# Four-stage network on one core: keys of two heads in one strip, a norm of a norm without its own moments, counts as thresholds, and a new order of the front

## The chip, the cores and the metric

The kernel runs on one core of a Trainium2 chip. The metric is the device time of the whole program in microseconds (us); lower is better. The core has five engines that run beside each other and wait for one another by semaphores: TensorE (PE; its weight loads are listed apart as PEld), VectorE (DVE), ScalarE (ACT), GpSimd (POOL) and SyncE (SP), which issues DMAs.

## The reference

The input is 16 sequences of 256 tokens with 128 features. Four blocks follow each other, each with a residual and a layer norm on both sides; `_layernorm` has no gain.

```python
x = x + _layernorm(_L0_attn_ref(_layernorm(x), ...))   # block 1: layer norm with gain, 16 heads of 8, MLP
x = x + _layernorm(_L0_ffn_ref(_layernorm(x), ...))    # block 2: dense MLP plus product-key experts
x = x + _layernorm(_L1_attn_ref(_layernorm(x), ...))   # block 3: 16 heads of 8, output bias
x = x + _layernorm(_L1_ffn_ref(_layernorm(x), ...))    # block 4: six layers of local attention and MLP
```

Block 1 begins with a second layer norm of what the first gives, so that a norm of a norm is computed. In block 2 each token has, for each of 4 query heads, two lists of 64 scores; the 8 best of each list are taken, the 64 sums of pairs are formed, the 8 best sums are kept, and the 8 experts with the indices `ix * 64 + iy` are mixed by a softmax of these sums. All arithmetic is fp32 in the reference.

## The kernel before

Blocks 1 to 3 are one software pipeline, called the front here; block 4 is another, which starts when the front has ended. A sequence lies as two tiles of 128 tokens, on partitions, by 128 features. The front's work on one sequence is cut into 177 named steps. The string `FRONT` lists them as `name:lag`. The loop `run` goes through this list once a pass; in pass number s it executes each step for sequence s minus its lag, if there is one. The text calls one pass a step of the pipeline where it gives times. With 16 sequences and a largest lag of 11 there are 27 passes. The class `InOrder` makes every engine run its instructions in exactly this order, and all instructions made through it carry the line of its helper, L46. So each engine has a queue of its own in the order of the list, and an instruction starts when those in front of it on its engine and those it needs are done.

The names, with the engine of each:

- La to Lh are the eight layer norms. `.a` takes the moments on DVE (two `bn_stats`, two `bn_aggr`), `.b` makes scale and offset on POOL (four instructions on 2 elements), `.c` applies them on ACT, `.d` adds to the residual on POOL. La and Lb are the two norms in front of block 1. Lc is inside block 1, Ld behind it; Le and Lf stand around block 2, Lg and Lh around block 3.
- A and C are the attentions of blocks 1 and 3. Small letters are PE, capitals what takes the result out of PSUM: q and k project, Q and K copy out on ACT, m and s are score products (each for 4 or 2 groups of heads; m finds the maxima, s is done again with the negated maxima added as a row), M is the maximum on DVE, n transposes the maxima on PE, N adds them to the queries on DVE, E is the exponential on ACT, c is the product with the values, C copies it on ACT, t and x transpose on PE, T divides by the sum on DVE, X copies on ACT, o is the output product.
- tA, tM, tB, tC are transposes on PE, TA to TC copies on ACT; h, H, mo, my is block 1's MLP (PE, ACT with Gelu, PE, DVE), hs the sum in front of it (DVE); xo and hb add bias rows on POOL; Cy adds the bias of block 3 on DVE.
- Block 2: S (PE) and Z (ACT) make the scores, r0 and r1 take the 8 best of each list on DVE (tiles `mx`, `mi`), r2 casts the indices (`mf`) and forms the sums of pairs, r3 takes the 8 best sums, shifts their places right by 3 (`pk<-pk`), casts them (`pa<-pk`) and subtracts the largest; r4 is the exponential on ACT, r5 the sum of it on DVE. r6 and r7 mark, by comparing and adding on 4096 elements a partition, the rank of each second index in `rt`; r8 counts for each first index how many partners were kept, and writes a threshold for each into `rt` (tiles `at`, `cnt`, `nb`, `thr`); r9 does the case of an index past the end (`far`, `pl`). b, B transpose `rt`; d multiplies with a constant matrix `sel`, and D keeps an expert's weight where the product is above a constant (tile `w`). ys and X0, X1 on POOL form the weights of all 512 experts from the scores (`exy<-sim,mx`; `w<-exy`, one for each tile of tokens), ye is the exponential on ACT between them. w multiplies with the experts' inner products on DVE (`w<-w,hh`), W applies Silu on ACT, l corrects one element on POOL, g, G, o, oy give the output; u, U, f, F are the dense products.

The 16 heads lie in four groups of four strips. A strip is 32 partitions, holds one head's 8 rows of keys or queries, and row `NMROW` takes the maxima.

## Time and profile before

| what | value |
|---|---|
| median of 3 runs | 4587.18 us (4584.28 to 4592.25) |
| the profiled execution | 4579.81 us, of which the span from first to last instruction is 4578.0 us |
| busy in the span | PE 93%, PEld 68%, DVE 73%, ACT 70%, POOL 67% |
| granted clock of TensorE | 0.973 of full speed |
| end of the front | the last residual sum of block 3, `x<-x,Lhy` on POOL, starts at 1250.61 us |

The page cuts the span into 40 slices, in each of which a digit gives an engine's busy share in tenths. The chain of waits goes back from the last instruction to what released each; the groups put instructions of one shape together, with the number, the busy time and the mean duration; the timeline lists instructions of one engine by start and duration. A duration in it includes time in which an instruction has been started and is held up, and the start of one may lie before the end of the one in front.

### The profile page before, as it was taken

Reading aid. Unit: us, or ns where it says so; the run is one execution under the profiler, and the core shown is the slowest. Engines: PE = TensorE matmul, PEld = TensorE weight load, DVE = VectorE, ACT = ScalarE, POOL = GpSimd, SP = SyncE. Lnnn points to the kernel's source line nnn. Section 1 sums busy time; section 2 is a strip of 40 time slices with the busy share of each in tenths; the row PEclk is TensorE's granted clock in tenths of the full one; section 3 lists DMA queues with packets and bytes.
Section 4 is the critical chain, followed back from the end, with each engine's and each line's share of the span. In section 5 each row is a group of like instructions: output and inputs, shape, how many; then the busy total and the mean of one; then the engine's idle time right before and its main releaser. Section 6 shows DMA issues by size and latency. Waiting matters only on the chain.

```text
span 4578.0 us, 169228 instructions
## 1 busy us (share of the span) xinstructions
PE 4275.8 (93%) x74304; PEld 3123.8 (68%) x74304; DVE 3334.8 (73%) x5376; ACT 3197.5 (70%) x5919; POOL 3072.3 (67%) x2858
## 2 busy tenths in 40 slices
PE   7799999998668999999999999999999999999997
PEld 5567676676435767777777777777777777777776
DVE  3899999998546776777767677776767777676774
ACT  2576676776467777777777777777777777777775
POOL 3343443443357887778777777778777787878885
PEclk9899999999879999999999999999999999999998
DMA  2000000000022322223232222323232232323231
GB/s 50 1 2 3 2 2 2 2 2 2 13 65 66 78 71 70 71 70 76 66 74 68 73 73 67 75 68 78 66 74 67 73 75 68 71 59 78 70 73 50
DMA packets 220132, 242.03 MB, mean 53 GB/s; under 512 B 95777, under 2 KB 126578, under 8 KB 219250
## 3 DMA queue, kind: packets, MB, share of 16 engines
q1 hardware_dynamic: 215170, 229.10, 20.4%
q8 instruction: 584, 9.57, 0.9%
q10 hardware_dynamic: 4224, 2.10, 0.2%
q14 instruction: 154, 1.26, 0.1%
...
## 4 chain that ended last, share of the span: by engine, by line
PE 64%; DVE 17%; ACT 12%; issue 2%; POOL 2%; DMA 1%; SPq 1%; ACTq 0%; POOLq 0%; DVEq 0%
PE pp L46 22%; PE po L46 11%; PE sc L46 6%; PE ph L46 6%; PE pt L46 5%; PE pc L46 5%; PE pe L46 3%; DVE m L46 3%; ACT qT L46 2%; DVE nmA L46 2%; ACT eT L46 2%; PE s L46 2%; ACT v L46 2%; ACT cT L46 2%; ACT xn L46 2%
## 5 line engine op out<-in xcount | busy, mean ns | idle before, releaser
L46 PE MATMUL pp<-part,xT 128*128 128x512 f32 x2304 | 1103.4, 609 | 18.3 <-ACT cT L46 9.7
L46 POOL TENSOR_TENSOR am<-a,r 128x1024 f32<-128x1024 f32 x384 | 730.2, 1902 | 435.1 <-PE pt L46 211.9
L46 POOL TENSOR_TENSOR a<-a 128x512 f32<-128x512 f32 x768 | 960.2, 1271 | 11.9 <-DVE a L46 11.9
L46 DVE TENSOR_TENSOR a<-pp,tab 128x2048 f32<-128x2048 f32 x384 | 877.6, 2285 | 118.8 <-POOL am L46 83.1
L46 PEld LDWEIGHTS pp<-part,xT 128*128 128x128 f32 x2304 | 404.7, 192 | 361.6 <-issue 300.5
L46 DVE TENSOR_TENSOR e<-sc,m_win 128x1024 f32<-128x1024 f32 x192 | 235.1, 1224 | 473.1 <-PE sc L46 469.8
L46 ACT COPY kT<-pt 128x512 f32<-128x512 f32 x384 | 229.1, 597 | 446.3 <-PE pt L46 443.8
L46 DVE TENSOR_REDUCE sm<-e 128x16 f32<-128x1024 f32 x192 | 233.2, 1215 | 382.3 <-ACT e L46 382.3
L46 POOL TENSOR_TENSOR e<-e,mx 128x1024 f32<-128x1024 f32 x192 | 365.1, 1901 | 208.1 <-DVE mx L46 202.7
L46 PEld LDWEIGHTS pt<-ident,am 128*128 128x128 f32 x3072 | 353.3, 141 | 204.8 <-issue 150.3
L46 PE MATMUL pt<-ident,am 128*128 128x128 f32 x3072 | 466.0, 279 | 25.5 <-POOL am L46 22.0
L46 ACT ACTIVATE sq<-pp 128x1024 f32<-128x1024 f32 x384 | 396.0, 1032 | 99.0 <-PE pp L46 69.0
L46 DVE TENSOR_REDUCE r<-sq 128x16 f32<-128x1024 f32 x384 | 455.9, 1208 | 0.0
...
L46 PEld LDWEIGHTS po<-wo,cT 128*128 128x128 f32 x3200 | 376.8, 193 | 57.6 <-issue 45.1
...
L46 PE MATMUL po<-wo,cT 128*128 128x128 f32 x3200 | 382.5, 277 | 5.2 <-ACT cT L46 5.2
L46 POOL TENSOR_TENSOR e<-e,sm 128x1024 f32<-128x1024 f32 x192 | 365.3, 1903 | 5.5 <-DVE sm L46 5.5
...
L46 ACT COPY eT<-pe 128x512 f32<-128x512 f32 x384 | 224.7, 585 | 78.5 <-PE pe L46 78.5
...
## 6 DMA issues: line engine op xcount, KB each, us to landing
...
```

What stands on the lines that cost most here:

```text
L46: ins = trace(*args, **kw)
```

## The change

Keys: the two halves of the heads share strips. A strip now holds the keys of two heads, in rows 0 to 7 and 8 to 15, and the maxima's row moves to 16. The key projection has two groups in place of four, and so have its copies out of PSUM. The queries keep four groups; each head's 8 rows stand at the place of its key, and the other 8 are zero, so a score product of 32 rows gives one head's scores.

The second norm: Lb no longer takes moments. The mean of a normed row is zero and its variance follows from La's moments and scale; Lb.b computes scale and offset from these with six instructions on POOL, and Lb.c applies them to `x` instead of to the first norm's result.

Thresholds: r8 writes the count itself into `rt`, as the result of its last reduce. The instruction that formed 8 minus the count is gone. `sel` has plus one where it had minus one, and D compares with 8.5 instead of 0.5.

Order: r3 is cut in two, and the shift, the cast and the subtraction become r3b, which stands behind Lf.a. The list `FRONT` is new: the lags are mostly larger by 3 or 4, since the list begins at another place of the pass, and several steps have moved against each other: among others w0 behind Le.a, W0 in front of Z0, Cs1 behind S1, ye behind oy, Lf.c behind AE0, and X1 behind Lf.d and La.b and ahead of Lg.b.

```diff
@@ -25,7 +25,9 @@
 NH = 16
 DH = 8
-NMROW = 8
+NMROW = 16
 RH, NK, NE, TOP = 4, 64, 512, 8
@@ -119,32 +121,31 @@
             )
         return m
-    def in_strips(self, pool, name, src, scale=1.0):
-        w = pool.tile([128, 4, 4, 32], FP, name=name)
+    def in_strips(self, pool, name, src, keys, scale=1.0):
+        w = pool.tile([128, 2 if keys else 4, 4, 32], FP, name=name)
         self.nc.gpsimd.memset(w, 0.0)
-        self.nc.vector.tensor_scalar(
-            w.rearrange("p g j s -> p (g j) s")[:, :, 0:DH],
-            src.rearrange("p (h e) -> p h e", e=DH),
-            scale,
-            None,
-            ALU.mult,
-        )
+        src = src.rearrange("p (k s j e) -> p s k j e", k=2, s=2, e=DH)
+        for s in range(2):
+            dst = w if keys else w.rearrange("p (k s) j r -> p s k j r", s=2)[:, s]
+            self.nc.vector.tensor_scalar(dst[:, :, :, DH * s : DH * s + DH], src[:, s], scale, None, ALU.mult)
         return w.rearrange("p g j s -> p g (j s)")
     FRONT = """
-F0:8 Lf.d:9 r7:8 Lg.a:9 Ak0:6 As2:7 r4:8 F1:8 Ak2:6 Ct0:10 AK0:6 Lg.b:9 AK2:6 r8:8 AE2:7 Ac0:7
-        Ct1:10 X1:8 Am0:6 Lb.c:5 Lh.c:11 CT0:10 AC0:7 r5:8 CT1:10 r9:8 Lg.c:9 Ac2:7 AM0:6 AC2:7 Lh.d:11 Av:6
-        tA:5 b0:8 AV:6 TA:5 b1:8 Cx:10 B0:8 At0:7 B1:8 AT0:7 CX:10 d02:8 At1:7 d00:8 D02:8 d10:8 AT1:7 D00:8
-        d13:8 D10:8 Am2:6 D13:8 tC:9 Ax:7 TC:9 AM2:6 Co:10 Cy:10 AX:7 d03:8 Ao:7 hs:7 Am1:6 D03:8 d12:8
-        Lc.a:7 Lc.b:7 D12:8 d01:8 Ck0:9 d11:8 La.c:4 CK0:9 D01:8 Cq0:9 Lc.c:7 tM:7 CQ0:9 D11:8 TM:7 Ck2:9
-        La.b:2 w0:8 Cq2:9 CK2:9 AM1:6 CQ2:9 h0:7 h2:7 Cm0:9 Cv:9 H0:7 w1:8 H2:7 mo:7 hb:7 W0:8 CM0:9 xo:5
-        CV:9 Cm1:9 my:7 Ld.a:7 u2:8 CM1:9 Ld.b:7 An0:6 l0:8 U2:8 AN0:6 Ld.c:7 Ld.d:7 An2:6 Le.a:7 Cm2:9
-        Cn0:9 Aq0:5 Le.b:7 W1:8 AN2:6 CN0:9 CM2:9 Lb.a:4 Le.c:7 AQ0:5 Aq2:5 tB:7 La.a:0 TB:7 Cs1:9 S0:7
-        AQ2:5 l1:8 S1:7 Z0:7 Cn2:9 Z1:7 Lh.a:10 Lb.b:4 CN2:9 r0:7 r1:7 g0:8 g1:8 r2:7 r6:7 CE1:9 G0:8 Cs0:9
-        G1:8 ys:7 o:8 CE0:9 oy:8 Lh.b:10 Cs2:9 CE2:9 u0:7 Lf.a:8 Cc0:9 U0:7 Cc2:9 Lf.b:8 ye:7 r3:7 As1:6
-        X0:7 AE1:6 f0:7 CC0:9 As0:6 Lf.c:8 CC2:9 AE0:6 f1:7
+        CM0:13 An2:10 Cv:13 W1:12 Cm1:13 my:11 Aq0:9 Ld.a:11 AN2:10 u2:12 Ld.b:11 CV:13 Ld.c:11 Aq2:9 CM1:13
+        Cm2:13 AQ0:9 Ld.d:11 U2:12 Le.a:11 w0:12 AQ2:9 Le.b:11 Le.c:11 CM2:13 tB:11 TB:11 Cn0:13 S0:11 l1:12
+        W0:12 S1:11 CN0:13 La.a:0 Z0:11 Cn2:13 Z1:11 Cs1:13 l0:12 Lh.a:14 CN2:13 r0:11 CE1:13 g0:12 g1:12
+        Lh.b:14 G0:12 r1:11 G1:12 Cs0:13 r2:11 Lh.c:14 r3:11 CE0:13 o:12 Cs2:13 u0:11 oy:12 ys:11 ye:11
+        Lf.a:12 Cc0:13 CE2:13 U0:11 Cc2:13 As1:10 r3b:11 r6:11 r4:11 X0:11 r5:11 Lf.b:12 CC0:13 f0:11 AE1:10
+        f1:11 r7:11 F0:11 As0:10 CC2:13 Ct0:13 Ct1:13 CT0:13 CT1:13 F1:11 AE0:10 Ak0:9 As2:10 Ak2:9 Lf.c:12
+        Lf.d:12 tA:8 AK0:9 r8:11 Ac0:10 AK2:9 Av:9 La.b:5 AE2:10 TA:8 Lb.c:7 Am0:9 Lg.a:12 AC0:10 Ac2:10
+        AV:9 r9:11 AM0:9 b0:11 AC2:10 X1:11 Cx:13 B0:11 b1:11 Lb.b:5 d02:11 CX:13 D02:11 At0:10 AT0:10 B1:11
+        At1:10 AT1:10 La.c:8 d13:11 d10:11 Lg.b:12 xo:8 D13:11 d00:11 Lg.c:12 D10:11 Am2:9 tC:12 Ax:10 TC:12
+        D00:11 Co:13 Ck0:12 AX:10 AM2:9 Ao:10 hs:10 Am1:9 CK0:12 Cy:13 Lc.a:10 d03:11 Ck2:12 CK2:12 Lc.b:10
+        D03:11 Lc.c:10 d12:11 D12:11 d01:11 d11:11 Cq0:12 hb:10 CQ0:12 D01:11 D11:11 tM:10 TM:10 AM1:9
+        Cq2:12 h0:10 CQ2:12 h2:10 w1:11 An0:9 H0:10 AN0:9 Cm0:12 H2:10 Lh.d:14 mo:10
...
@@ -182,7 +183,7 @@
         a = w["A"] = {
             "qb": self.load(wp, "qb", ins["q_b"], [128, 4]),
-            "kb": self.load(wp, "kb", ins["k_b"], [128, 4]),
+            "kb": self.load(wp, "kb", ins["k_b"], [128, 2]),
         }
         nc.vector.tensor_scalar(a["qb"], a["qb"], DH**-0.5, None, ALU.mult)
         w["f1"] = wp.tile([128, 4, 128], FP, name="f1")
@@ -208,7 +209,7 @@
                     a["wv"] = wp.tile([128, 128], FP, name="wv")
                     nc.vector.tensor_copy(a["wv"], p)
                 else:
-                    a[f"w{k}"] = self.in_strips(wp, f"w{k}", p, DH**-0.5 if k == "q" else 1.0)
+                    a[f"w{k}"] = self.in_strips(wp, f"w{k}", p, k == "k", DH**-0.5 if k == "q" else 1.0)
             u = self.load(fp, "uo", ins["out_U"], [96, 128])
             v = self.load(fp, "vo", ins["L0_attn_out_V"], [96, 128])
             p = ps.tile([128, 128], FP, name="p", tag="f")
@@ -247,14 +248,14 @@
             c = w["C"] = {
                 "qb": None,
-                "kb": self.load(wp, "no_kb", ins["no_kb"], [128, 4]),
+                "kb": self.load(wp, "no_kb", ins["no_kb"], [128, 2]),
                 "ob": self.load(wp, "bo", ins["L1_attn_bo"].partition_broadcast(128), [128, D]),
                 "wv": self.load(wp, "wv3", ins["L1_attn_Wv"], [128, 128]),
                 "wo": self.load(wp, "wo3", ins["L1_attn_Wo"], [128, 128]),
             }
             for k in "qk":
                 raw = self.load(fp, f"raw{k}", ins[f"L1_attn_W{k}"], [128, 128])
-                c[f"w{k}"] = self.in_strips(wp, f"w3{k}", raw, DH**-0.5 if k == "q" else 1.0)
+                c[f"w{k}"] = self.in_strips(wp, f"w3{k}", raw, k == "k", DH**-0.5 if k == "q" else 1.0)
         w["up"] = self.load(wp, "wup", ins["W_up"], [128, 512])
         w["dn"] = self.load(wp, "wdn", ins["W_down"].rearrange("(c p) d -> p c d", p=128), [128, 4, D])
         w["de"] = self.load(wp, "de", ins["down_embed"], [128, NE])
@@ -271,9 +272,7 @@
         sel = w["sel"] = wp.tile([128, 8, NK], BF, name="sel")
         nc.vector.tensor_copy(sel[0:64], self.ident_bf[0:64, 0:64].unsqueeze(1).to_broadcast([64, 8, NK]))
-        nc.vector.tensor_scalar(
-            sel[64:72], self.ident_bf[64:72, 64:72].unsqueeze(2).to_broadcast([8, 8, NK]), -1.0, None, ALU.mult
-        )
+        nc.vector.tensor_copy(sel[64:72], self.ident_bf[64:72, 64:72].unsqueeze(2).to_broadcast([8, 8, NK]))
         w["m_q"] = self.mask(wp, "m_q", [128, 4, 128], [(0, 1, [[0, 4], [-1, 128]])])
         w["m_k"] = self.mask(wp, "m_k", [128, 4, 128], [(0, -1, [[0, 4], [1, 128]])])
@@ -333,7 +332,7 @@
             @op(name + ".a")
             def _(n):
                 st = small(name + "st", [2, 6])
-                mv = put(n, (name, "mv"), small(name + "mv", [2, 2]))
+                mv = put(n, (name, "mv"), small(name + "mv", [2, 2], bufs=6))
                 src = source(n)
                 for t in range(2):
                     nc.vector.bn_stats(st[:, t, :], src[:, t, :])
@@ -343,8 +342,8 @@
             @op(name + ".b")
             def _(n):
                 mv = get(n, (name, "mv"))
-                rstd = put(n, (name, "rstd"), small(name + "rstd", [2]))
-                off = put(n, (name, "off"), small(name + "off", [2]))
+                rstd = put(n, (name, "rstd"), small(name + "rstd", [2], bufs=6))
+                off = put(n, (name, "off"), small(name + "off", [2], bufs=6))
                 nc.gpsimd.tensor_scalar(rstd, mv[:, :, 1], EPS, None, ALU.add)
                 nc.gpsimd.tensor_tensor(rstd, rstd, self.half.to_broadcast([128, 2]), ALU.pow)
                 nc.gpsimd.tensor_scalar(off, mv[:, :, 0], -1.0, None, ALU.mult)
@@ -369,7 +368,21 @@
                 nc.gpsimd.tensor_tensor(x_of(n), x_of(n), get(n, name + "y"), ALU.add)
         norm("La", x_of, tile_as("x0", 3))
-        norm("Lb", lambda n: get(n, "x0"), tile_as("x1", 2, "turned"))
+        norm("Lb", x_of, tile_as("x1", 2, "turned"))
+        @op("Lb.b")
+        def _(n):
+            mv, first = get(n, ("La", "mv")), get(n, ("La", "rstd"))
+            scale, off = put(n, ("Lb", "rstd"), small("Lbrstd", [2])), put(n, ("Lb", "off"), small("Lboff", [2]))
+            r = small("Lbr", [2])
+            nc.gpsimd.tensor_tensor(r, mv[:, :, 1], first, ALU.mult)
+            nc.gpsimd.tensor_tensor(r, r, first, ALU.mult)
+            nc.gpsimd.tensor_scalar(r, r, EPS, None, ALU.add)
+            nc.gpsimd.tensor_tensor(r, r, self.half.to_broadcast([128, 2]), ALU.pow)
+            nc.gpsimd.tensor_tensor(scale, first, r, ALU.mult)
+            nc.gpsimd.tensor_tensor(off, get(n, ("La", "off")), r, ALU.mult)
         norm("Lc", lambda n: get(n, "hs"), tile_as("x2", 2, "turned"))
         norm("Ld", lambda n: get(n, "y"), tile_as("Ldy"))
         norm("Le", x_of, tile_as("xn", 2, "turned"))
@@ -418,8 +431,8 @@
                         r = slice(32 * j, 32 * j + 32)
                         nc.tensor.matmul(
                             s[:, i, o : o + 128],
-                            lhsT=lhs[r, g, lcols],
-                            rhs=rhs[r, g, rcols.start + o : rcols.start + o + 128],
+                            lhsT=lhs[r, g * lhs.shape[1] // 4, lcols],
+                            rhs=rhs[r, g * rhs.shape[1] // 4, rcols.start + o : rcols.start + o + 128],
                             start=False,
                             stop=i == m - 1 and o == 512 // m - 128,
                         )
@@ -430,16 +443,15 @@
             nm, va = a["nm"], a["va"]
             pairs = {"0": 0, "2": 2}
-            def projected(n, g, weights, name):
-                p = put(n, (k + name, g), bank("p" + name, [2, SEQ]))
-                for i in range(2):
-                    nc.tensor.matmul(
-                        p[:, i, :], lhsT=weights[:, g + i, :], rhs=get(n, "xT" + k), start=True, stop=True
-                    )
+            def projected(n, g, weights, name, m):
+                p = put(n, (k + name, g), bank("p" + name, [m, SEQ]))
+                for i in range(m):
+                    lhsT = weights[:, g * m // 2 + i, :]
+                    nc.tensor.matmul(p[:, i, :], lhsT=lhsT, rhs=get(n, "xT" + k), start=True, stop=True)
             @by(k + "q", pairs)
             def _(n, g):
-                projected(n, g, a["wq"], "q")
+                projected(n, g, a["wq"], "q", 2)
             @by(k + "Q", pairs)
             def _(n, g):
@@ -455,16 +467,14 @@
             @by(k + "k", pairs)
             def _(n, g):
-                projected(n, g, a["wk"], "k")
+                projected(n, g, a["wk"], "k", 1)
             @by(k + "K", pairs)
             def _(n, g):
                 if g == 0:
-                    put(n, k + "kT", pool.tile([128, 4, SEQ], FP, name="kT" + k))
+                    put(n, k + "kT", pool.tile([128, 2, SEQ], FP, name="kT" + k))
                 kT, p = get(n, k + "kT"), get(n, (k + "k", g))
-                for i in range(2):
-                    bias = a["kb"][:, g + i : g + i + 1]
-                    nc.scalar.activation(kT[:, g + i, :], p[:, i, :], AF.Identity, bias=bias)
+                nc.scalar.activation(kT[:, g // 2, :], p[:, 0, :], AF.Identity, bias=a["kb"][:, g // 2 : g // 2 + 1])
             @op(k + "v")
             def _(n):
@@ -710,6 +720,11 @@
             for g in range(G):
                 nc.vector.max(sc[:, g, :], pairs[:, g, :])
                 nc.vector.max_index(pk[:, g, :], sc[:, g, :], pairs[:, g, :])
+            put(n, "pk", pk), put(n, "sc", sc)
+        @op("r3b")
+        def _(n):
+            pk, sc = get(n, "pk"), get(n, "sc")
             nc.vector.tensor_scalar(pk, pk, 3, None, ALU.logical_shift_right)
             nc.vector.tensor_copy(put(n, "pa", small("pa", [G, TOP], BF, bufs=1)), pk)
@@ -755,9 +770,8 @@
             m8 = small("m8", [G, 8, TOP], BF, bufs=1)
             nc.vector.tensor_tensor(m8, rows(get(n, "mf")[:, 0], 8), each(w["i8"]), ALU.is_equal)
             nc.vector.tensor_tensor(m8, m8, rows(nb, 8), ALU.mult)
-            thr = small("thr", [G, 8], bufs=1)
-            nc.vector.tensor_reduce(thr, m8, AX.X, ALU.add)
-            nc.vector.tensor_scalar(get(n, "rt")[:, :, NK:NR], thr, -1.0, 8.0, ALU.mult, ALU.add)
+            with tc.nc.allow_low_precision("whole numbers up to 8"):
+                nc.vector.tensor_reduce(get(n, "rt")[:, :, NK:NR], m8, AX.X, ALU.add)
         @op("r9")
         def _(n):
@@ -819,7 +833,7 @@
         def _(n, t, h):
             v = get(n, ("w", t))[:, h, :]
-            nc.vector.scalar_tensor_tensor(v, get(n, ("d", t, h)), 0.5, v, ALU.is_gt, ALU.mult)
+            nc.vector.scalar_tensor_tensor(v, get(n, ("d", t, h)), 8.5, v, ALU.is_gt, ALU.mult)
         @by("w", tiles)
         def _(n, t):
...
```

More of the change, by code (lines that the diff above doesn't have):

```diff
@@ L1451, in local_masks, with strips @@
         return masks
-def strips(v, one):
-    w = np.zeros((4, 32, 4), np.float32)
+def strips(v, keys):
+    w = np.zeros((4, 32, 2, 2), np.float32)
     if v is not None:
-        w[:, :DH, :] = v.reshape(4, 4, DH).transpose(1, 2, 0)
-    if one:
-        w[:, NMROW, :] = 1.0
-    return w.reshape(128, 4)
+        v = v.reshape(2, 2, 4, DH)
+        for s in range(2):
+            w[:, DH * s : DH * s + DH, :, s] = v[:, s].transpose(1, 2, 0)
+    w = w.reshape(128, 2, 2)
+    if not keys:
+        return w.reshape(128, 4)
+    w = w.sum(2)
+    w[NMROW::32] = 1.0
+    return w
 def rotary():
```

## The prediction

> **What bounds the kernel now.** I read the slices of the page first, then the busy time of a stretch of the front, the chain of waits through one step of it, the groups by shape, and last the instructions of VectorE and of GpSimd in order of time through the same step. In the slices the kernel falls into two parts.
>
> ```profile
> PE   7799999998668999999999999999999999999997
> ...
> DVE  3899999998546776777767677776767777676774
> ...
> POOL 3343443443357887778777777778777787878885
> ```
>
> A slice is 4578.0 / 40 = 114 us. The fourth block, from slice 12 on, is bound by PE and is not touched; its 3.3 ms stay. The front (blocks 1 to 3, up to about 1250 us) shows PE and DVE both at nine tenths. The next rows are the busy time of 700 us of it (PE, PE's weight loads, DVE, ACT, POOL), pieces of the chain of one step, and a row of the waits between 200 and 1100 us.
>
> ```profile
> 300.00:1000.00 700.00, 653.01 (x7859) 484.46 (x7857) 655.97 (x1791) 502.62 (x1021) 292.11 (x429) 0.97 0.01 2
> ```
>
> ```profile
> 547.83 2.92 DVE rt L46
> ...
> 600.48 2.29 DVE m L46
> 616.84 2.92 DVE rt L46
> ```
>
> ```profile
> PE pc L46 <- DVE z L46: 35.4, 12, 3.0
> ```
>
> The same instruction comes back after 69.0 us (1165.48 less 547.83, nine steps, gives 68.6): a step is 68.6 us, and DVE is busy 94% of it, PE 93%. Of the two, DVE sets the step. The chain inside it runs over DVE rows almost throughout, and PE stands 3.0 us a step behind DVE just where DVE is held. It is held here (VectorE, then GpSimd, in order of time; start, duration):
>
> ```profile
> 588.75 0.69 DVE L46 TENSOR_TENSOR qaC<-pn,qTC 128x512 f32<-128x512 f32 x1 [1.61 <-PE pn L46]
> ...
> 607.06 2.09 DVE L46 TENSOR_SCALAR pk<-pk 128x64 uint32<-128x64 uint32 x1
> 609.18 0.65 DVE L46 CAST pa<-pk 128x64 bf16<-128x64 uint32 x1
> ...
> 615.10 0.20 DVE L46 CAST nb<-cnt 128x64 bf16<-128x64 f32 x1
> ...
> 616.12 0.69 DVE L46 TENSOR_REDUCE thr<-m 128x64 f32<-128x512 bf16 x1
> 616.84 2.92 DVE L46 TENSOR_SCALAR rt<-thr 128x64 bf16<-128x64 f32 x1
> ```
>
> ```profile
> 567.03 2.30 POOL L46 TENSOR_SCALAR Larstd<-Lamv 128x2 f32<-128x2 f32 x1
> ...
> 598.40 2.61 POOL L46 TENSOR_TENSOR Lhrstd<-Lhrstd,half 128x2 f32<-128x2 f32 x1
> ...
> 605.48 3.62 POOL L46 TENSOR_TENSOR w<-exy 128x2048 f32<-128x2048 f32 x1 [0.42 <-ACT exy L46]
> ...
> 616.10 3.61 POOL L46 TENSOR_TENSOR w<-exy 128x2048 f32<-128x2048 f32 x1
> ```
>
> Three DVE instructions on 64 elements take 2.09, 0.65 and 2.92 us where a cast of the same size takes 0.20. The first ends with POOL's first 3.6 us product (X0), the third with the second (X1): 605.48 + 3.62 = 609.10, 616.10 + 3.61 = 619.71. The maxima and the reduce that ran beside the same products kept their 0.21 and 0.69 us. It works the other way too: a POOL instruction on 2 elements takes 2.30 us beside DVE's `w<-w,hh`.
>
> **The change part by part**, in us a step.
>
> The removed instruction. `rt<-thr` is gone, and the next DVE instruction began 2.84 after it: -2.84. The reduce writes bf16 instead of fp32, the sign moves into `sel` and a constant, at nothing.
>
> The norm of a norm. Two `bn_stats` and two `bn_aggr` of Lb leave DVE; from the start of Lb's first to the start of La's first it is 585.27 to 585.88: -0.61. POOL's Lb.b grows from four small instructions to six of 0.2 to 0.7 us, on an engine busy 42% of the stretch: nothing, since Lb.c is due two steps later. Without that cover it would cost 0.4.
>
> Keys two heads a strip. The projection `pk` halves: PE wrote it with 120 matmuls in 32.0 us for the second attention and 96 in 25.9 for the first, so 8 a sequence of 0.27 each, and 2 x 1.07 go from PE. On ACT four of eight `kT` activations of 0.47 go, about 1.7. Neither engine sets the step; at the two ends, where a lone sequence goes through the chain, it gives about 2 us once. The score matmuls keep count and shape, because the queries lie in the same strips with zeros for the other head. The setup gets one small DVE instruction more for each of four weights (0.29 each, behind the loads): nothing.
>
> The new order, X0 against r3b. `pk<-pk` and `pa` are now their own step r3b, behind Lf.a. I count from T, the end of r1. DVE does r2 (1.4), r3 without its tail (eight times 0.45) and Lf.a (0.65): r3b is ready at T+5.6. X0 waits for `ye`, which stands behind `oy` on ACT, and `oy` for PE: between the end of S1 and the output product, PE does Cn2 0.45, Cs1 1.6 (newly here), g0 and g1 3.5, Cs0 2.1 and the product itself 3.7, in all about 11. S1 ends about 2 before r0 starts, and r0 and r1 take 7.3, so `oy` ends near T+2.1, `ye` near T+2.8, and X0 runs to T+6.5. It still holds the shift, by 0.9 instead of 1.9: -1.0. For `pa`, whose 0.58 to the next start become 0.2, -0.4, as Lf.d (0.73, the POOL instruction that held it) has moved away. Bounds of both together: -2.3 if X0 is early, 0 if it is 1 us later than I count. The cast `mf`, 0.86 beside POOL's `exy`, stands as before: 0.
>
> X1. It is behind Lf.d and La.b in POOL's queue and waits for neither r8 nor AM0, so its start is that of Lf.d plus 2.1 (0.73 and four small instructions of 1.35). Lf.d waits for Lf.c on ACT, which now stands behind CE2 2.07, U0 with a table load 1.9, r4 with a load 1.6, CC0 0.6, AE1 2.05, F0 0.65, CC2 0.6, F1 0.65 and AE0 2.05; starting from Cs2 at T+3.3 and with Lf.c's own 0.9 that is T+16.4. So X1 runs from T+18.5 to T+22.1. DVE is then at: r3b done T+7.1, r6 4.5, r5 0.4, r7 3.4, CT0 and CT1 1.0, r8 2.8, Lg.a 0.6, that is `far`, a TENSOR_SCALAR on 64 elements and the like of the removed one, at T+19.8. By the count it waits 2.3. Bounds: 0, if X1 starts under AM0, 4 later; +3.3, if X1 gets in ahead of the product `m<-m,nb` in r8. The count leaves out every wait of nine ACT instructions in a row, and waits move X1 towards AM0; I take 1.7, nearer to the count.
>
> A rule is to be weighed here. The Trainium skill, page "SBUF — State Buffer", section "Who interferes with whom", says that VectorE and GpSimd share one port pair, that whoever issues first has it for the whole instruction, and that a VectorE instruction with two SBUF inputs contends with a GpSimd instruction that reads SBUF. By that letter POOL's small norm instructions would hold DVE as well: Lf.b and La.b, 2 x 1.5, now fall on r6, r7 and r8, all with two SBUF inputs, which would add up to 3 a step and eat the gain. The rows differ. `Lhrstd` ran until 601.01, and the product that DVE began at 600.48 still took its usual 2.29; the wait was POOL's, 2.61 for 0.71. By the row it is 0, and I take the row. For the long products the rule and the rows agree, and it is the rule's list that makes `far` the next victim.
>
> Waits. New in front of the first maxima (r0): `w0` now stands right behind Le.a and takes the port before Le.b, as `Larstd` above shows. From the end of Le.a: Le.b held 2.2 and 1.6 of its own, Le.c 0.9, tB and TB 0.8, then W0 on ACT ahead of Z0, 3.1, and Z0 0.7: r0 can start at 9.3. DVE fills `w0` 2.3, CM2 2.5, CN0 0.7, La.a and Lh.a 1.2, CN2 0.7 = 7.4. It waits 1.9, against 1.61 in the row at 588.75: +0.3. Lh.b in turn no longer lies beside r6. The other waits of DVE (0.35 before Le.a, and those behind PE) I leave; a queue other than these gets no DMA more or less, since the front issues none in its steps.
>
> Sum: -2.84 - 0.61 - 1.0 - 0.4 + 1.7 + 0.3 = -2.85. Sixteen sequences pass at this pace (from hs of the first at 91 us to that of the last at 1111, and one step more): -46, and -2 at the ends: -48. The largest lag grows from 11 to 14, but the three steps in front hold only La.a, 0.6 each, while DVE has nothing else: nothing. The profiled execution took 4579.81 us (span 4578.0), 7.4 under the median of the runs, 4587.18. It would become 4532; of the median, 4539.
>
> **The rivals.**
>
> All collisions gone. Then -2.84 - 0.61 - 1.9 - 0.4 and no other loss: -5.75 a step, with the ends -94, 4493. For it: the parts that moved (Lf.a before r3b, X1 behind Lf.d) are those that keep the products beside maxima and PSUM work. Against it: no dependence holds X1 back.
>
> PE is the bound. It is busy 93%. Then what counts is the 2.1 of `pk`: -34 and 4553. Against it: the row in which PE waits 3.0 for DVE.
>
> The lock only finds other victims: X0 holds the shift as before and X1 the product in r8. Then -2.84 - 0.61 + 3.3 + 0.3 = +0.2 a step: about 4588, no difference.
>
> Slower: r0 comes too late. The chain behind Le.a is serial: if Cm2 (1.8) also stands in front of tB and W0 pays a table load (1.28), r0 starts at 12.4, and every further hold of Le.b by DVE adds up to 2.2; two of them give 16.8, a wait of 9.4. It decides from a wait of 1.9 + 2.85 = 4.75 on; at 5.75 a step costs 1 more than now, 4603. For it: W0 before Z0 and `w0` before Le.b are both new. Against it: the functions queued on ACT from W1 to W0 need no second load.
>
> **How the numbers follow.** My forecast 0.42, all collisions gone 0.25, PE the bound 0.12, other victims 0.09, slower 0.12. A measurement of this kernel tells about 0.2%, 9 us, from no change. Faster takes the first three and 0.04 of the fourth, 0.83; same 0.05; slower 0.12. The range runs from 4475 (under it a twentieth, of the second case) to 4583, short of most of "other victims" and of "slower".
>
> **What would show it.** Right: a step near 65.8 us between two r9; no row `rt<-thr`; `Lbst` gone; `kT` activations at half their count; `pk<-pk` near 1.1 us and `far` near 2; a wait near 1.9 before the first `mx`. Wrong: `far`, `at` or `m<-m,nb` at 3 us or more; `mx` waiting more than 5; or a step above 68.6 with PE rows on the chain.

## The result, and the profile after

The changed kernel is slower: 4616.64 us (4614.14 to 4619.67, 4 runs) against 4585.73 (4582.00 to 4592.25) for the kernel before on the same chip, a ratio on record of 1.0073 with a 95% interval of 1.0060 to 1.0085 (the two medians alone give 1.0067). The forecast was 4539, with a range up to 4583.

All instructions made through the helper now carry L48. Slices, after:

```profile
PE   6798999988758999999999999999999999999997
...
DVE  3888888888635777767676767777676767677774
...
POOL 4434434434246888778777877777877777778885
```

In slices 3 to 9 VectorE (DVE) has eights where there were nines, and TensorE (PE) has eights in slices 4 and 9. It is the front, and neither engine is fuller. The front's last residual sum, `x<-x,Lhy`, starts at 1291.85 us where it started at 1250.61, and what lies behind it takes as long as before (3325 us from its end, 3327 before). The busy time of the same 700 us (PE, PEld, DVE, ACT, POOL, then the granted clock) says it in numbers:

```profile
300.00:1000.00 700.00, 634.76 (x7499) 464.90 (x7539) 618.12 (x1679) 475.99 (x952) 285.89 (x415) 0.93 0.01 2
```

DVE is busy 88% where it was 94%, and TensorE's clock is 0.93 of full speed where it was 0.97. A step (the mean of nine, from the last instruction of one r9 to that of a later one) went from 68.74 to 71.35 us. I added up, between these marks, the time of each kind of instruction and the idle time in front of it. DVE's work fell from 64.4 to 62.7 a step; its idle time doubled, from 4.3 to 8.7. So work was saved, and more than that was lost in waits. (0.26 of the fall in work is La.a: with r9 at lag 11 and La.a at lag 0, it has no sequence left in these nine steps.) The waits between 200 and 1100 us (total, times, longest), after:

```profile
PE xTp L48 <- ACT xn L48: 38.3, 12, 3.3
DVE qaC L48 <- PE pn L48: 36.9, 22, 3.0
PE d L48 <- DVE w L48: 32.9, 13, 3.0
...
DVE nmA L48 <- PE s L48: 22.7, 13, 1.8
```

and the same four before (the 35.4 us of `pc` behind `z`, shown with the prediction, are gone):

```profile
DVE qaC L46 <- PE pn L46: 26.3, 13, 2.8
PE xTp L46 <- ACT xn L46: 7.9, 13, 2.2
DVE nmA L46 <- PE s L46: 4.3, 13, 1.8
...
PE d L46 <- DVE w L46: 2.4, 12, 0.2
```

PE waits in two new places, before tB (`xTp<-xn`) and before the third `d`; DVE waits behind PE in two, before CN0 and CN2 (`qaC`) and before AM2 (`nmA`). Each PE wait is followed by a DVE wait.

**The first place.** POOL, DVE and PE in order of time after Le.a (start, duration, idle before):

```profile
597.74 2.16 POOL L48 TENSOR_SCALAR Lerstd<-Lemv 128x2 f32<-128x2 f32 x1 [0.82 <-DVE Lemv L48]
```

```profile
597.57 2.26 DVE L48 TENSOR_TENSOR w<-w,hh 128x2048 f32<-128x2048 f32 x1
599.74 2.48 DVE L48 TENSOR_REDUCE nmC<-s 128x2 f32<-128x512 f32 x4
603.66 0.69 DVE L48 TENSOR_TENSOR qaC<-pn,qTC 128x512 f32<-128x512 f32 x1 [1.45 <-PE pn L48]
...
607.93 0.69 DVE L48 TENSOR_TENSOR qaC<-pn,qTC 128x512 f32<-128x512 f32 x1 [2.96 <-PE pn L48]
608.54 0.22 DVE L48 MAX8 mx<-sim 128x8 f32<-128x64 f32 x1
```

```profile
601.85 0.86 PE L48 MATMUL xTp<-ident,xn 128*128 128x128 f32 x2 [3.15 <-ACT xn L48]
602.50 1.06 PE L48 MATMUL pn<-ident,nmC 128*128 128x128 f32 x4
603.35 3.62 PE L48 MATMUL psim<-wsim,xTB 128*128 128x512 f32 x4
```

w0 has the port and holds Lerstd for 2.16, as forecast. Then comes what was not: PE has nothing for 3.15 us, and after that `psim` takes 3.62 where the kernel before has 1.98. The stretches show why (columns as above):

```profile
597.00:602.00 5.00, 1.84 (x38) 1.42 (x36) 5.00 (x9) 1.75 (x5) 3.44 (x5) 0.93 0.00 0
602.00:607.00 5.00, 5.00 (x12) 2.60 (x13) 1.52 (x6) 3.77 (x9) 0.89 (x3) 0.50 0.00 0
607.00:612.00 5.00, 5.00 (x63) 4.47 (x62) 3.79 (x24) 4.29 (x7) 0.65 (x3) 0.89 0.02 5
...
641.00:646.00 5.00, 2.43 (x13) 1.14 (x13) 4.86 (x13) 2.19 (x6) 2.39 (x8) 0.96 0.00 0
646.00:650.00 4.00, 4.00 (x46) 3.24 (x44) 2.24 (x5) 0.37 (x1) 0.00 (x0) 0.62 0.00 0
```

In the second row PE is busy all of the time at a clock of 0.50. Cn0 and Cn2, which DVE needs for CN0 and CN2, stand in PE's queue behind tB and around this `psim`. r0 begins 10.9 us after the end of Le.a in this step (608.54 less 597.65) and 10.2 in the mean of the nine; before it was 7.6.

**The second place** is the last two rows. Their 0.96 and 0.62 are means: in the same trace cut finer, the clock is full up to 645.64, half up to 649.05, and full again.

```profile
642.25:645.63 3.38, 0.81 (x4) 0.14 (x3) 3.31 (x9) 0.94 (x3) 1.30 (x4) 1.00 0.00 0
645.65:649.04 3.39, 3.39 (x38) 2.36 (x38) 1.67 (x3) 0.00 (x0) 0.00 (x0) 0.50 0.00 0
649.06:652.00 2.94, 2.92 (x27) 2.27 (x30) 2.92 (x6) 1.22 (x3) 0.00 (x0) 1.00 0.02 6
```

X1 now holds another DVE instruction:

```profile
635.54 3.61 POOL L48 TENSOR_TENSOR w<-exy 128x2048 f32<-128x2048 f32 x1
```

```profile
621.73 1.95 DVE L48 TENSOR_SCALAR pk<-pk 128x64 uint32<-128x64 uint32 x1
...
635.56 0.69 DVE L48 TENSOR_REDUCE rt<-m 128x64 bf16<-128x512 bf16 x1
...
636.77 2.42 DVE L48 TENSOR_SCALAR far<-mf 128x64 bf16<-128x64 bf16 x1
...
846.78 2.77 DVE L48 CAST nb<-cnt 128x64 bf16<-128x64 f32 x1
```

`far` is held up to the step at 778 us; in the five steps from 847 on X1 comes earlier and holds `nb` in r8 (row at 846.78), with `far` free at 0.15. POOL's rows from Lf.d to X1, in a step of each kind, show why:

```profile
773.69 0.72 POOL L48 TENSOR_TENSOR x<-x,Lfy 128x256 f32<-128x256 f32 x1 [3.85 <-ACT Lfy L48]
...
776.45 3.62 POOL L48 TENSOR_TENSOR w<-exy 128x2048 f32<-128x2048 f32 x1
...
845.02 0.72 POOL L48 TENSOR_TENSOR x<-x,Lfy 128x256 f32<-128x256 f32 x1 [3.84 <-ACT Lfy L48]
845.70 3.80 POOL L48 TENSOR_TENSOR w<-exy 128x2048 f32<-128x2048 f32 x1
```

In the first step the four instructions of La.b stand between the two. La.b has lag 5 and r9 lag 11, so from the eleventh r9 on La.b has no sequence left, and X1 starts 0.7 us after Lf.d instead of 2.8. Either way AM0 and D02 are late. The third `d` needs a PSUM bank that D02 has to free:

```profile
644.61 1.58 PE L48 MATMUL d<-sel,rT 72*128 72x512 bf16 x3 [2.35 <-DVE w L48]
...
646.97 2.09 PE L48 MATMUL s<-kTA,qTA 32*128 32x128 f32 x32
```

and Am2's 32 scores, for which AM2 waits, take 2.09; the same 32 take 1.17 elsewhere in the step.

### The profile page after: what moved, and what is told of

The parts are those of the page before. It is cut to its first block, busy times and chain, and to the rows that moved or that the text cites. A ratio compares the mean times of both kernels' runs of the same rounds, so it can differ in the third digit from the quotient of the medians.

```text
span 4617.8 us, 168888 instructions
## 1 busy us (share of the span) xinstructions
PE 4276.7 (93%) x74116; PEld 3118.8 (68%) x74176; DVE 3309.9 (72%) x5300; ACT 3178.9 (69%) x5858; POOL 3094.3 (67%) x2890
## 4 chain that ended last, share of the span: by engine, by line
PE 68%; DVE 16%; ACT 11%; POOL 2%; issue 2%; DMA 1%; SPq 0%; POOLq 0%; ACTq 0%; DVEq 0%
PE pp L48 22%; PE po L48 12%; PE sc L48 6%; PE ph L48 6%; PE pt L48 5%; PE pc L48 5%; PE pe L48 3%; DVE m L48 3%; PE s L48 2%; ACT eT L48 2%; ACT qT L48 2%; ACT v L48 2%; ACT cT L48 2%; DVE mi L48 2%; ACT xn L48 2%
## 5 line engine op out<-in xcount | busy, mean ns | idle before, releaser
L48 PE MATMUL pp<-part,xT 128*128 128x512 f32 x2304 | 1100.8, 607 | 17.8 <-ACT cT L48 8.8
L48 POOL TENSOR_TENSOR am<-a,r 128x1024 f32<-128x1024 f32 x384 | 730.3, 1902 | 433.4 <-PE pt L48 215.7
L48 POOL TENSOR_TENSOR a<-a 128x512 f32<-128x512 f32 x768 | 960.6, 1272 | 11.7 <-DVE a L48 11.7
L48 DVE TENSOR_TENSOR a<-pp,tab 128x2048 f32<-128x2048 f32 x384 | 877.6, 2285 | 120.3 <-POOL am L48 84.2
L48 PEld LDWEIGHTS pp<-part,xT 128*128 128x128 f32 x2304 | 403.8, 192 | 360.8 <-issue 298.4
L48 DVE TENSOR_TENSOR e<-sc,m_win 128x1024 f32<-128x1024 f32 x192 | 234.9, 1224 | 474.3 <-PE sc L48 474.3
L48 ACT COPY kT<-pt 128x512 f32<-128x512 f32 x384 | 228.9, 596 | 446.5 <-PE pt L48 444.2
L48 DVE TENSOR_REDUCE sm<-e 128x16 f32<-128x1024 f32 x192 | 233.2, 1215 | 379.0 <-ACT e L48 379.0
L48 POOL TENSOR_TENSOR e<-e,mx 128x1024 f32<-128x1024 f32 x192 | 365.1, 1901 | 207.9 <-DVE mx L48 204.7
L48 PEld LDWEIGHTS pt<-ident,am 128*128 128x128 f32 x3072 | 352.9, 141 | 204.2 <-issue 149.0
L48 PE MATMUL pt<-ident,am 128*128 128x128 f32 x3072 | 465.8, 279 | 25.8 <-POOL am L48 22.0
L48 ACT ACTIVATE sq<-pp 128x1024 f32<-128x1024 f32 x384 | 395.9, 1031 | 98.5 <-PE pp L48 74.7
L48 DVE TENSOR_REDUCE r<-sq 128x16 f32<-128x1024 f32 x384 | 455.8, 1208 | 0.0
L48 PE MATMUL pc<-eT,vw 64*64 64x32 f32 x24576 | 439.9, 221 | 9.8 <-ACT eT L48 5.1
L48 PEld LDWEIGHTS pc<-eT,vw 64*64 64x64 f32 x24576 | 396.3, 135 | 75.2 <-issue 69.1
L48 PEld LDWEIGHTS po<-wo,cT 128*128 128x128 f32 x3200 | 382.4, 195 | 53.5 <-issue 45.0
L48 PE MATMUL po<-wo,cT 128*128 128x128 f32 x3200 | 387.2, 278 | 1.5 <-ACT cT L48 1.4
L48 POOL TENSOR_TENSOR e<-e,sm 128x1024 f32<-128x1024 f32 x192 | 365.4, 1903 | 5.0 <-DVE sm L48 5.0
L48 PE MATMUL sc<-kT,qT 64*32 64x64 f32 x24576 | 332.3, 224 | 4.2 <-DVE e L48 3.4
L48 PEld LDWEIGHTS sc<-kT,qT 64*32 64x32 f32 x24576 | 269.8, 105 | 80.3 <-issue 53.3
L48 ACT COPY eT<-pe 128x512 f32<-128x512 f32 x384 | 224.9, 586 | 76.6 <-PE pe L48 76.6
```

Of the source, the lines that this page charges most:

```text
L48: ins = trace(*args, **kw)
```

## The experiments

The theory after this comparison: the two long products on the shared port delay the way to PE (w0 through Le.b, X1 through D02), PE then stands still for 2.4 to 3.2 us, and what follows on it runs at half the clock in front of the instructions for which DVE waits. Rivals: the parts themselves bring nothing; only the delay counts and not the clock; another chain sets the step anyway. Each kernel is told as its difference from the changed one, or from one named; code cuts are marked by three dots.

| kernel | time, us | ratio to the kernel before (95%) | step, us |
|---|---|---|---|
| before | | 1 | 68.74 |
| changed | 4616.64 | 1.0073 (1.0060 to 1.0085) | 71.35 |
| 1 parts, old order | 4582.61 | 1.0007 (0.9998 to 1.0015) | 69.35 |
| 2 w0 behind CM2 | 4573.80 | 0.9983 (0.9975 to 0.9991) | 68.34 |
| 3 and W0 behind Z1 | 4579.57 | 0.9995 (0.9986 to 1.0004) | 68.35 |
| 4 r9 behind AM0 | 4599.11 | 1.0039 (1.0025 to 1.0053) | 70.23 |
| 5 w0 behind CM2, X1 behind Lg.b | 4544.17 | 0.9916 (0.9900 to 0.9933) | 65.87 |
| 6 filling ahead of tB | 4585.48 | 1.0008 (1.0001 to 1.0015) | 69.34 |
| 7 and in front of d | 4560.52 | 0.9957 (0.9940 to 0.9973) | 67.42 |
| 8 parts, old order, r9 late | 4553.75 | 0.9936 (0.9920 to 0.9953) | 66.93 |
| 9 as 5, r9 behind r8 | 4539.67 | 0.9908 (0.9891 to 0.9924) | 65.21 |
| 10 as 9, W0 behind Z1, ye ahead of oy | 4521.17 | 0.9868 (0.9852 to 0.9885) | 64.00 |
| 11 as 5, thresholds undone | 4549.43 | 0.9934 (0.9918 to 0.9951) | 66.24 |
| 12 as 5, keys undone | 4557.52 | 0.9947 (0.9930 to 0.9964) | 66.62 |

The kernel before took 4581.4 to 4581.9 beside kernels 1 to 12.

**Kernel 1: the parts in the old order.** Keys, norm and thresholds of the changed kernel, with the list of the kernel before (without Lb.a; r3b directly behind r3).

```diff
-... ys:11 ye:11 Lf.a:12 Cc0:13 CE2:13 U0:11 Cc2:13 As1:10 r3b:11 r6:11 r4:11 X0:11 ...
+... Lf.a:8 Cc0:9 U0:7 Cc2:9 Lf.b:8 ye:7 r3:7 r3b:7 As1:6 X0:7 ...
```

> The changed kernel's keys, norm and thresholds with the order of before (r3b directly behind r3, Lb.a left out of the list). Theory 'order': the three parts are a gain and the new order alone makes the kernel slower. Then a step loses the 2.84 us of the removed instruction and 0.61 of Lb's moments, and X1 holds the next VectorE instruction with the port, far, by about 1.6: step 66.7 us, 4550 us, ratio 0.992. Theory 'parts': the packed keys or the longer norm on POOL cost more than they save: step 70 or more, over 4600 us.

The time is that of the kernel before: the parts alone bring nothing here. Neither expectation came out, since at 69.35 the step lies between the 66.7 of the first and the 70 of the second. `rt<-thr` left DVE, -2.92, and Lb's moments, -0.54; but X1, which had held `rt<-thr`, now held `far` (+1.55) and `at<-at,far` (+0.47). And PE's 3 us of standing still, which in the kernel before lie ahead of `pc`, moved ahead of `d`:

```profile
623.84 1.70 PE L48 MATMUL d<-sel,rT 72*128 72x512 bf16 x3 [3.12 <-DVE cx L48]
...
626.32 2.09 PE L48 MATMUL s<-kTA,qTA 32*128 32x128 f32 x32
```

```profile
621.00:624.00 3.00, 0.17 (x1) 0.11 (x2) 2.97 (x7) 0.00 (x0) 0.00 (x0) 0.99 0.00 0
624.00:628.00 4.00, 3.95 (x39) 2.27 (x37) 2.62 (x6) 0.00 (x0) 0.00 (x0) 0.50 0.00 0
```

The half clock was in the kernel before as well. The stretch behind its wait for `z` reads

```profile
552.00:556.00 4.00, 3.98 (x42) 2.92 (x34) 3.86 (x9) 1.38 (x4) 0.00 (x0) 0.63 0.00 0
```

but there it slowed `pc` (3.80 a step against 2.95 in kernel 1), whose reader is a copy on ACT; before `rec`, the next DVE instruction on that path, DVE idled 0.16 a step. In front of `d` it slows Am2, and DVE's wait before the maxima grew from 0.21 to 1.75.

**Kernel 2: w0 behind CM2.**

```diff
-U2:12 Le.a:11 w0:12 AQ2:9 Le.b:11 Le.c:11 CM2:13 tB:11 ...
+U2:12 Le.a:11 AQ2:9 Le.b:11 Le.c:11 CM2:13 w0:12 tB:11 ...
```

> The changed kernel with one step moved: w0 behind CM2 instead of directly behind Le.a on VectorE. Theory 'port and clock': w0 holds POOL's Le.b by 2.2 us, so PE stands idle for 3.2 us in front of tB, its clock falls to half, and psim takes 3.6 instead of 2.0. Without it Lerstd falls from 2.2 to 0.2 us, the granted clock stays at 1.0 there, psim takes 2.0, and r0 starts about 8.7 us after the end of Le.a instead of 10.9: step -2.2, 4581 us, ratio 0.999. Theory 'queue': W0 ahead of Z0 on ScalarE is what makes r0 late, the hold of Le.b is hidden: no change, 4610 to 4620.

One name moved by four places gives back about 40 us of the changed kernel's time and makes it a little faster than the kernel before. The wait before tB fell from 3.23 to 1.30 a step, `psim` from 3.44 to 1.98, the wait before CN0 and CN2 from 3.70 to 0.21. The step fell by 3.0, where the theory had 2.2, as X0 came earlier too and `pk` fell from 1.69 to 0.28. Two smaller waits took their place: `mx` for Z0 1.29, CM2 1.0 more.

**Kernel 3: W0 behind Z1 as well.**

```diff
-Cn0:13 S0:11 l1:12 W0:12 S1:11 CN0:13 La.a:0 Z0:11 Cn2:13 Z1:11 Cs1:13 ...
+Cn0:13 S0:11 l1:12 S1:11 CN0:13 La.a:0 Z0:11 Cn2:13 Z1:11 W0:12 Cs1:13 ...
```

> As the last, and W0 behind Z1 on ScalarE as well. Theory 'port and clock': r0 starts when VectorE reaches it, about 6.8 us after Le.a; step -4.1 against the changed kernel, 4552 us, ratio 0.993. Theory 'queue': the whole gain of 2 to 4 us a step comes here and none of it in the run that moves w0 alone. A third outcome: the later W0 delays g0 and the dense output on PE, oy and with it Lf.a wait: the gain stays under 1 us against the run before.

The time is that of the third outcome, under 1 us a step, but not by its cause: the wait for Z0 went, 1.29, and `pk` was held again, 0.28 to 1.70, so the step is the same. What started the maxima earlier moved r3b into X0, since X0 did not come earlier with them. Kernel 10 takes this up.

**Kernel 4: r9 behind AM0** (w0 as in the change).

```diff
-AV:9 r9:11 AM0:9 b0:11 AC2:10 X1:11 ...
+AV:9 AM0:9 r9:11 b0:11 AC2:10 X1:11 ...
```

> The changed kernel with r9 behind AM0 on VectorE, so that POOL's second product X1 runs beside Lg.a and AM0, which read PSUM or one tensor. Theory 'port and clock': far and nb fall to 0.2 us (from 2.42 or 2.77), PE's wait of 2.8 us in front of d02 goes and with it the half clock in Am2, so that the wait in front of AM2 falls from 1.7 to 0.4: step -2.3 to -3.6, 4560 to 4580 us. Theory 'next victim': X1 only holds another instruction (m<-m,nb, at or pl) by as much: no change, 4610 to 4620.

`far` went from 1.33 to 0.09 a step, but 1.12 of a step was won, half of the least that was expected. `nb` stayed at 1.34, since in the later steps X1 holds it and r9's place changes nothing there: the third to the ninth step fell from 71.1 to 69.3 in the mean, the eleventh to the thirteenth from 71.7 to 71.5 only. The wait of `nmA` even rose, 1.74 to 2.10; r9 now stood between AM0 and D02, and PE still waited 2.09 ahead of `d`. To take X1 out of `far`'s way alone is half a cure.

**Kernel 5: w0 behind CM2, Lg.b ahead of X1, r9 behind D00.** Lg.b needs Lg.a on DVE, so X1 can't begin before r8 is through.

```diff
-AV:9 r9:11 AM0:9 b0:11 AC2:10 X1:11 ... d10:11 Lg.b:12 xo:8 ... D00:11 Co:13
+AV:9 AM0:9 b0:11 AC2:10 Lg.b:12 X1:11 ... d10:11 xo:8 ... D00:11 r9:11 Co:13
```

> The changed kernel with w0 behind CM2, Lg.b ahead of X1 on POOL, and r9 behind D00 on VectorE. X1 can then start only when r8 and Lg.a are done, and runs beside AM0 and the D's, which read PSUM. With w0 behind CM2 alone a step was 68.34 us, in which far took 1.33 and nb 1.34 (0.09 and 0.20 free), and VectorE waited 1.15 before the maxima AM0 and AM2. Port theory with the clock: far and nb go back, -2.4 of VectorE's time; D02 comes 2 to 3 us earlier, PE's 2.9 us before d fall to about 1, its matmuls after it keep the full clock, the wait of nmA shrinks. Step 65.5 to 66.3, time 4530 to 4545. Rival (another engine or another chain sets the step by now): the 2.4 turn into new waits of VectorE for PE, step 67.5 to 68.3, time 4560 to 4574.

As the theory had it, within the step and time it named. POOL's row of X1 and DVE's rows:

```profile
670.85 3.62 POOL L48 TENSOR_TENSOR w<-exy 128x2048 f32<-128x2048 f32 x1
```

```profile
666.91 0.19 DVE L48 CAST nb<-cnt 128x64 bf16<-128x64 f32 x1
...
670.36 1.29 DVE L48 TENSOR_REDUCE nmA<-s 128x4 f32<-128x512 f32 x2 [1.13 <-PE s L48]
```

X1 now lies under the maxima, which keep their pace. `far` 0.09, `nb` 0.19; the wait ahead of `d` fell to 0.33 a step, from 2.77 in the changed kernel and 2.87 in kernel 2. The two moves on X1 and r9 came together here; kernel 9, in which r9 stands elsewhere, still has `far` and `nb` free.

**Kernels 6 and 7: the clock alone.** The changed kernel with its order untouched; tB (and in kernel 7 also At1) first writes its bank with matmuls on ready data, which the transposes then overwrite.

```diff
 def _(n):  # tB
     src, p = get(n, key), put(n, "p" + name, bank("xTp", [2, 128]))
+    for _ in range(6 if name == "B" else 0):
+        nc.tensor.matmul(p, lhsT=w["f1"][:, 0, :], rhs=w["up"][:, 0:256], start=True, stop=True)
...
 def _(n, t):  # t0 and t1 of A and C, kernel 7
     cs = get(n, k + "cs")
+    for _ in range(5 if k == "A" and t == 1 else 0):
+        nc.tensor.matmul(p.rearrange("p h e -> p (h e)")[:, 0:256], lhsT=w["f1"][:, 0, :],
+                         rhs=w["up"][:, 0:256], start=True, stop=True)
```

> The changed kernel, order untouched; tB writes its bank first with six matmuls of 128x256 on ready data (about 0.43 us each, 2.6 us in all, and overwritten by the transposes), which lie in the 3.2 us in which PE has nothing to do. It tells the clock from the wait: xn comes as late as before. Clock theory: the granted clock stays near 1, psim takes 2.0 instead of 3.44 us, the pn behind it 0.6 instead of 0.87, r0 starts 1.7 us earlier, step 71.35 to about 69.7, time about 4590. Rival (only the lateness of xn counts, and psim is slow for another reason): psim stays at 3.4, time 4616 or a little more.

> The same, and five such matmuls (2.1 us) in At1's bank ahead of its transposes, in the time in which PE waits 2.8 us for D02 before the third d. Clock theory: the score matmuls of Am2 take 1.17 instead of 2.09, the wait before the maxima AM2 falls by about 1, step 0.7 to 1.2 below the kernel with the filling in tB alone, 12 to 20 us. Rival: the maxima wait for something else or AT1, which becomes late by the filling, takes it back: within 4 us of that kernel, or slower.

More work on PE made the kernel faster, by 0.65% (1.0073 to 1.0008) and by a further 0.5%, the second more than the 12 to 20 us that were expected. PE in kernel 6 (each of the six matmuls in fp32 counts as two rows of the trace):

```profile
651.01 2.86 PE L48 MATMUL xTp<-wup,f 128*128 128x256 f32 x12
654.24 0.71 PE L48 MATMUL xTp<-ident,xn 128*128 128x128 f32 x2 [0.37 <-ACT xn L48]
...
655.42 1.98 PE L48 MATMUL psim<-wsim,xTB 128*128 128x512 f32 x4
```

The transposes of `xn` still start 3.2 us behind the scores in front, as in the changed kernel; only the gap is filled. But `psim` is back at 1.98 and the stretch reads

```profile
654.00:658.00 4.00, 3.68 (x17) 2.20 (x18) 1.97 (x8) 3.58 (x9) 0.00 (x0) 1.00 0.00 0
```

The wait before CN0 and CN2 fell from 3.70 to 2.03 a step, which is the 2.01 of the kernel before, and r0 begins 8.6 us after Le.a instead of 10.2. In kernel 7 the scores of Am2 take 1.17 again and the wait of `nmA` is 0.21, again that of the kernel before:

```profile
609.83 2.42 PE L48 MATMUL pt<-wup,f 128*128 128x256 f32 x10
...
614.61 1.17 PE L48 MATMUL s<-kTA,qTA 32*128 32x128 f32 x32
```

There is no stretch at half the clock between 300 and 1000 us in kernel 7. The rest of DVE's work stood as in the changed kernel: 62.7 and 62.6 a step, with `far` and `nb` held at 1.33 and 1.34, and `pk` at 1.59. So the clock, not the delay by itself, cost about 30 us in the first place and 25 in the second. The Trainium skill, page "TensorE: Matmul & The Clock Gate", Part 1, says that TensorE goes to half its clock after at least one idle window of about 3.4 us; the halving to 0.50 is in the rows, but here gaps of 3.15 and 2.35 us were enough, so for this kernel the measured, shorter gap decides.

**Kernel 8: the parts in the old order, r9 behind D13.**

```diff
-... CT1:10 r9:8 Lg.c:9 Ac2:7 AM0:6 ... Am2:6 D13:8 tC:9
+... CT1:10 Lg.c:9 Ac2:7 AM0:6 ... Am2:6 D13:8 r9:8 tC:9
```

> Keys, norm and thresholds of the changed kernel in the old order (4582.6 so far, step 69.35), with r9 moved from in front of AM0 to behind D13. far took 1.64 there beside X1, at 0.47, and PE waited 3.46 before d and then ran Am2 at half the clock. Port and clock theory: far goes back to 0.09, AM0 and D02 come 2 us or more earlier, PE's wait before d falls to about 1.5 and Am2 takes 1.17: step 66.8 to 67.5, time 4540 to 4555. Rival (the parts bring nothing in the old order, since PE or the order of maxima and scores sets the step): step 69 or more, time 4578 to 4585.

As expected: with one name moved, the old order with the parts is 28 us faster than the kernel before. (The move was not tried without the parts.) `far` fell by 1.55 and `at<-at,far` by 0.47, the wait ahead of `d` from 3.46 to 0.72, that of `nmA` from 1.75 to nothing.

**Kernel 9: as kernel 5, with r9 between r8 and Lg.a.**

```diff
-r8:11 Ac0:10 ... D00:11 r9:11 Co:13
+r8:11 r9:11 Ac0:10 ... D00:11 Co:13
```

> The version with w0 behind CM2 and X1 behind Lg.b (step 65.87), with r9 not behind D00 but between r8 and Lg.a. VectorE waited there 1.13 us before AM0 and 0.82 before D02, with r9's 2.2 us standing where nothing waits. Now r9 fills these waits, and X1, held back by Lg.a through Lg.b, still starts only under AM0. Port theory: far stays at 0.1, the waits before AM0 and D02 go, step 64.0 to 64.8, time 4505 to 4525. Rival (D02 and AM2 wait for PE, which is moved back by as much, or X1 now runs later and holds the copies of another product): step 65.5 to 66.2, time 4538 to 4550.

Half of the expected step was won, and the time lies in the rival's range: the wait before AM0 went (1.08 to 0), that before the D's grew (1.14 to 1.61). 4.5 us between overlapping intervals is not a difference that these runs show.

**Kernel 10: as kernel 9, W0 behind Z1, ys and ye ahead of oy.**

```diff
-S0:11 l1:12 W0:12 S1:11 CN0:13 La.a:0 Z0:11 Cn2:13 Z1:11 ... u0:11 oy:12 ys:11 ye:11 Lf.a:12
+S0:11 l1:12 S1:11 CN0:13 La.a:0 Z0:11 Cn2:13 Z1:11 W0:12 ... u0:11 ys:11 ye:11 oy:12 Lf.a:12
```

> The same, with W0 behind Z1 on ScalarE (r0 waited 1.29 us for Z0, which stood behind W0's 2.56) and ye ahead of oy, so that X0 starts as soon as the maxima of both lists are there. With W0 behind Z1 but ye behind oy, in an earlier run, pk was held 1.7 by X0 and nothing was gained. If that was the cause: pk free at 0.3, no wait before the maxima, a step 0.8 to 1.3 below the run beside it, 13 to 20 us. If pw, which needs W0, sets the chain now: within 5 us of it.

The step fell by 1.21, as expected: the wait of 1.29 is gone and `pk` stays free at 0.12, though `nb` takes 0.61 again where it took 0.19. It is the fastest of all, 1.3% below the kernel before.

```profile
300.00:1000.00 700.00, 673.58 (x8354) 491.77 (x8354) 647.37 (x1860) 521.07 (x1042) 288.65 (x450) 0.99 0.01 2
```

DVE is busy 92% and PE 96% of the time, at a clock of 0.99.

**Kernel 11: as kernel 5, thresholds undone.**

```diff
+            thr = small("thr", [G, 8], bufs=1)
+            nc.vector.tensor_reduce(thr, m8, AX.X, ALU.add)
+            nc.vector.tensor_scalar(get(n, "rt")[:, :, NK:NR], thr, -1.0, 8.0, ALU.mult, ALU.add)
-                nc.vector.tensor_reduce(get(n, "rt")[:, :, NK:NR], m8, AX.X, ALU.add)
```

> The version with w0 behind CM2 and X1 behind Lg.b (4544.2, step 65.87), with the thresholds as before: rt<-thr back, thr in fp32, sel with minus one, 0.5 in D. If the 2.92 us of rt<-thr were only X1's hold, it takes 0.15 to 0.25 here, since X1 starts later: step +0.1 to +0.2, time +1 to +4. If it is slow by itself: step +2.5 to +2.9, time about 4590.

`sel` and the constant in D went back with it. A row of the groups of this kernel (count, busy time, mean ns):

```profile
L48 DVE TENSOR_SCALAR rt<-thr 128x64 bf16<-128x64 f32 x15 | 2.9, 195 | 0.5
```

195 ns where it took 2923 before: all but 0.2 of its cost was X1's hold. The step grew by 0.37, more than the 0.2 expected (`far` took 0.11 more); the 5 us by which the time grew lie within overlapping intervals.

**Kernel 12: as kernel 5, keys undone** (four groups of strips, 8 `pk` matmuls a sequence and attention in place of 4).

```diff
-NMROW = 16
+NMROW = 8
...
-                projected(n, g, a["wk"], "k", 1)
+                projected(n, g, a["wk"], "k")
...
-                nc.scalar.activation(kT[:, g // 2, :], p[:, 0, :], AF.Identity, bias=a["kb"][:, g // 2 : g // 2 + 1])
+                for i in range(2):
+                    bias = a["kb"][:, g + i : g + i + 1]
+                    nc.scalar.activation(kT[:, g + i, :], p[:, i, :], AF.Identity, bias=bias)
```

> The same version with the keys as before, four groups of strips with one head each: PE has 2.1 us a step more for pk, ScalarE 1.7. Prediction's reading (neither sets the step): within 8 us of 4544.2. Rival (PE, with 4.5 us idle in a step of 65.87, is on the chain at AM0 and AM2, for which VectorE waits): step +1 to +2, time 4560 to 4578.

13 us and 0.75 a step, between the two expectations. The projections took 1.6 us more on PE, and DVE's wait before its AM0 and AM2 rose from 1.08 to 1.70. ScalarE's copies of the keys took 1.5 more as well, so the two engines' shares were not told apart; PE's idle time did not grow (4.5 to 4.3), which speaks for PE. In this order, in which `far` and `nb` are free, part of the projections' time counts.

## Why the prediction was wrong

**The savings were right.** The removed `rt<-thr` gave 2.92 (forecast 2.84), Lb's moments 0.54 (0.61), `pa` 0.46 (0.4). Kernel 11 adds what the forecast didn't say: the 2.92 were a hold, not a cost, and an order in which X1 waits for r8 gives nearly all of it without the edit.

**X0 against r3b: 0.4, not 1.0.** `pk` fell from 2.08 to 1.69. In the step shown r1 ended at 615.98, so X0, which ended at 623.63, ran to T+7.65, where the count had T+6.5. The bound "0 if it is 1 us later than I count" was the right one to look at.

**X1: 2.4, not 1.7.** X1 began at T+19.6 (count 18.5), `far` came at T+20.8 (count 19.8), and the hold of 2.42 is the count's own 2.3. To shade it to 1.7 for waits on ACT was wrong, and so was the one place: in the later steps it is `nb`, held for 2.77, close to the upper bound's case. The count took La.b's four instructions ahead of X1 for granted, and the later steps have none. X1 held something in the kernel before and in kernels 1 to 4, 6 and 7; in kernel 8, where no dependence holds it back either, it held nothing, because r9 had moved away.

**The wait before r0: +1.7, not +0.3.** This is the largest term, with the next. The chain was seen (Lerstd held for 2.2, measured 2.16), and with the clock kept up (kernel 6) the wait is 2.03 against the 2.01 before, so the wait was counted right but for the clock (r0 begins at 8.6 there where the count had 9.3, and DVE fills less of it). This is the step that failed: it priced S0, S1 and the transposes behind a 3 us gap at the durations that they had without one.

**"The other waits of DVE I leave": +1.5 before AM2, and 1.5 more in three small ones.** This term stood at nothing, for no reason given. The wait before AM2 is the clock's again, since kernel 7 takes it back to 0.21. The small ones are `hs` 0.59, `w<-d,w` 0.47 and `nmC` 0.43; kernel 7 removed the first, and the other two were not told apart.

The sum a step by the trace is -2.92 - 0.54 - 0.40 - 0.46 + 2.39 + 1.69 + 1.53 + 1.49 = +2.78, against +2.61 measured; the rest is in small rows, La.a's -0.26 among them.

**The factor and the ends.** The two profiled executions differ by 39.9 us (4619.67 less 4579.81), the medians by 30.9. In the traces the end of the front moves by 41.2: 31.9 of it lie between the first r9 and the last, fifteen steps of 2.1 in the mean, 4.1 ahead of the first and 5.3 behind the last. The forecast had sixteen steps of the middle's size and -2 at the ends. The 9.4 at the ends were not in it, and with tB filled (kernel 6) they are gone, at -0.7. For kernels 5 and 7 to 12 the time won is 11 to 16 times the step won, so the middle's step times sixteen is an upper estimate.

**PE as a bound** was dismissed for "the row in which PE waits 3.0 for DVE". The row is right and the conclusion was too quick. A wait of PE isn't spare time when what follows it runs at half the clock in front of something that DVE needs; where it lies decides. "Neither engine sets the step", the reason for keys at nothing, holds no longer once DVE is not held: undoing the keys cost 13 us in kernel 12, of PE's time or ScalarE's. In the changed order itself the keys were not undone.

**The rivals.** "r0 comes too late" had the sign, the place and the first cause, Le.b behind w0. It asked for Cm2 in front of tB, a table load and further holds of Le.b to get to 4603; the trace needed none of these, and the clock made 4617. "The lock only finds other victims" was true of X1, in kernel 1 too, and would have given no difference by itself. "All collisions gone" needed moves that the change does not have: in kernel 10 `pk` and `far` are free and the step is 64.0.

What stays open: what causes the waits before `w<-d,w` and `nmC`. The norm was not tried alone; its 0.54 is read from the trace.
